# A graph-network kernel on one core: an adding transfer and a norm's use moved to later steps of the first stage

## The chip, the cores and the metric

The kernel runs on one core of a Trainium2 chip. The core has five engines that run side by side, each through its own stream of instructions in order: TensorE (PE in the profile; PEld is its weight load), VectorE (DVE), ScalarE (ACT), GpSimd (POOL) and SyncE (SP). Transfers are issued from POOL's, SP's or ACT's stream and carried out by 16 DMA engines. The metric is the time of one execution on the device, in microseconds; lower is better.

## What is computed

Four layers stand one after the other; each adds its result to its input and normalises every row of 256 values to mean 0 and variance 1. The first layer, the one that the change touches, is

```
h = relu(S @ (x @ W1)); h = relu(S @ (h @ W2)); y = S @ (h @ W3)    # S = adj * adj, 64x64
x = layernorm(x + y)          # (x - mean) / sqrt(var + 1e-5), over 256 values
```

with x of 128 x 64 x 256 values, W1 256x512, W2 512x1024, W3 1024x256, all in float32. The second layer needs the eigenvectors of a 64x64 Laplacian made from adj, applies them before and after a small two-layer network, the third holds two graph convolutions and LSTMs over windows of 1 to 4 nodes, and the fourth an attention over the graph.

## The kernel before

The 8192 rows are 64 tiles of 128 rows, in 16 groups of four tiles. The first stage (layer0) loops over the groups; layers two to four follow as a second stage, whose order a planner (class Plan, with costs and slots) decides.

**The first stage.** Each of the three products with a weight is done in the seven products of Strassen's scheme instead of eight. A generator, seven, gives one product each time that it is called by next: w2 (two of them) for the second weight, w3 for the third, w1 for the first weight of the next group. Their orders are 1, 2, 6, 5, 7, 3, 4 (w1, and w2 but for the last two) and 1, 2, 5, 6, 7, 3, 4 (w3). The result of a product is copied by ScalarE or added by VectorE out of a PSUM bank in the step after it.

The sums of operands that Strassen's scheme needs for the third weight are in the tile sh with four slots. They are made by transfers: less has ScalarE write a negated block into a slot, a plain transfer from SP copies a block, and adds (L1055) issues from POOL a transfer that adds its source to its destination. Slot 3 becomes the sum of a negated block and slot 1, and is read by w3's product 3; slot 1 is itself the result of two adding transfers.

**Steps.** The function step (L1020) is called once behind each product: it runs what is pending, that is the copy or addition of the product before, takes in a new pending piece, and then runs one piece from the list norms, if there is one:

```
if norms:
    norms.pop(0)()
```

Pieces come from mix_rows (L1122 to L1140), which multiplies by S, adds to x and puts the pieces of one half group's row norm on the list: scalar_norm (L808) gives two means (total with Identity), two sums of squares (total with Square), root (three small POOL instructions, L819 to L821) and two apply (ScalarE, L824). For the second half a piece for storing the rows follows (L1141).

**What sets the order.** Under tc.manual_schedule the streams of TensorE, VectorE and ScalarE keep the order in which the code calls them. POOL and SP are not in that list in this stage's block (it names three engines); the framework orders their streams when the program is built. The eigenvalue work of the second layer (function eigen) is spread between the products by an estimate of time; it uses TensorE, VectorE (lines L52 and L312 in the profile) and ScalarE (L385, L397) up to about 800 us.

**The hand-over.** What is left on the list norms at the end of the first stage is given to the planner of the second by left_over, one piece behind the other.

Of the kernel before, what the change touches and what calls it, by code (L numbers as in the profile page):

```python
# [12 lines left out]
AF = mybir.ActivationFunctionType  # L13
# [791 lines left out]
                                op0=ALU.subtract, op1=ALU.mult)  # L805


def scalar_norm(tc, pool, x, half, spare):  # L808


    nc = tc.nc
    S, G = nc.scalar, nc.gpsimd
    nm, va, rs, nb = (pool.tile([P, 2], F32, name=f"sn_{n}") for n in ("nm", "va", "rs", "nb"))

    def total(out, t, func, **kw):
        S.activation(spare[0](), x[:, t, :], func, accum_out=out[:, t:t + 1], **kw)

    def root():
        G.tensor_scalar(rs, va, 1.0 / D, EPS, op0=ALU.mult, op1=ALU.add)  # L819
        G.tensor_tensor(rs, rs, half[:, :2], ALU.pow)  # L820
        G.tensor_tensor(nb, nm, rs, ALU.mult)  # L821

    def apply(t):
        S.activation(x[:, t, :], x[:, t, :], AF.Identity, bias=nb[:, t:t + 1], scale=rs[:, t:t + 1])  # L824

    return ([lambda t=t: total(nm, t, AF.Identity, scale=-1.0 / D) for t in range(2)] +
            [lambda t=t: total(va, t, AF.Square, bias=nm[:, t:t + 1]) for t in range(2)] + [root] +
            [lambda t=t: apply(t) for t in range(2)])


# [6 lines left out]
def kernel(  # L837
# [58 lines left out]
    def rows_of(g):  # L896

        return X[:, 4 * g:4 * g + 4, :] if g < RING else XA[:, 4 * (g - RING):4 * (g - RING) + 4, :]
# [61 lines left out]
    eig, norms, due = [], [], [float("inf")]  # L960
# [44 lines left out]
    sh = pa.tile([P, 4, 4, 256], F32, name="sh")  # L1005
# [15 lines left out]
    def step(then=None):  # L1021

        while pending:
            pending.pop(0)()
        if then:
            pending.append(then)
        if norms:
            norms.pop(0)()
# [4 lines left out]
    def sums_of_weights(w, b12):  # L1033
        yield VL.tensor_sub(w[7], w[3], b12)
        yield VL.tensor_sub(w[5], b12, w[1])
        yield VL.tensor_sub(w[6], w[3], w[5])
        yield VL.tensor_sub(w[4], w[2], w[6])
# [9 lines left out]
    def sums_first():  # L1047
        VL.tensor_add(sx[:, 0], X21, X22)
        VL.tensor_sub(sx[:, 1], sx[:, 0], X11)
        VL.tensor_sub(X21, X11, X21)  # L1050

    def less(slot, j, c):
        S.activation(sh[:, slot, 2 * j:2 * j + 2], h2[:, 0, 4 * c + 2 * j:4 * c + 2 * j + 2, :], AF.Identity, scale=-1.0)

    def adds(out, src):  # L1055
        nc.gpsimd.dma_start(out, src, accum_op=ALU.add)  # L1056

    def burst(dst, src, c):
        to = dst.rearrange("p c (t h n) -> p h c t n", h=2, n=N)
        p = [bank().rearrange("p (c t n) -> p c t n", c=2, t=4) for _ in range(2)]  # L1060
        for t in range(4):
            for k in range(2):
                for m, f, h, hs in quads(c + k):
                    PE.matmul(p[h][m, k, t, :], src[hs, t, f], sqT2[hs, hs], start=True, stop=True)  # L1064
        now[0] += QUADS
        between()

        def result():
            for h in range(2):
                S.copy(to[:, h, c:c + 2], p[h])  # L1070

        step(result)
# [6 lines left out]
    def by_second(j):  # L1079

        def product(out, i, new):
            w, a = (x[i] for x in second)
            chained(out, [[(w[:, k, c * P:(c + 1) * P], a[:, k, :]) for k in range(2)] for c in (2 * j, 2 * j + 1)], new)

        return product
# [9 lines left out]
    def seven(n, product, c11, c12, c21, c22, last, order=(1, 2, 6, 5, 7, 3, 4)):  # L1095

        def view(b):
            return b[:, :2 * n].rearrange("p (i n) -> p i n", i=2)

        def add(dst, b):  # L1100
            VL.tensor_add(dst, dst, b)
            if last is relu:
                relu(dst, dst)

        ch = view(bank("ch"))
        for i in order:
            if i in (2, 5):
                b = view(bank("ps" if i == 2 else "b5"))
                b2, b5 = (b, None) if i == 2 else (b2, b)
            out = {2: b2 if i == 2 else None, 5: b5 if i == 5 else None, 3: b5 if i == 3 else None}.get(i, ch)  # L1110
            product(out, i, i in (1, 2, 5))
            step({1: lambda: S.copy(c11, ch), 2: lambda: add(c11, b2), 6: lambda: S.copy(c12, ch),
                  5: lambda: S.copy(c22, b5), 7: lambda: add(c22, ch), 3: lambda: add(c12, b5),
                  4: lambda: last(c21, ch)}[i])
            yield i
# [11 lines left out]
    def weigh(t):  # L1127
        p = bank()
        run(p, [(m1[:, k, t * P:(t + 1) * P], aw1[:, k, :]) for k in range(2)])
        step(lambda: relu(h1[:, t, :], p))  # L1130
# [14 lines left out]
    def sums_second():  # L1145
        S1, S2, S4 = (ss[:, i] for i in range(3))
        VL.tensor_add(S1, A21, A22)
        VL.tensor_sub(S2, S1, A11)
        VL.tensor_sub(A21, A11, A21)
        VL.tensor_sub(S4, A12, S2)  # L1150

    def layer0():
        n = NT // 4
        burst(m1, rows_of(order[0]), 0)
        step()
        for t in range(4):
            weigh(t)
            if t == 1:
                for _ in sums_of_weights(second[0], B12):
                    pass  # L1160
        step()
        for c in (0, 2):
            burst(m2, h1, c)
            step()
        for g in range(n):
            last = g == n - 1
            then = {} if last else {
                (1, 1): lambda: less(2, 0, 0),
                (1, 6): lambda: sums_first() if g else burst(m1, rows_of(order[1]), 0),
                (0, 5): lambda: (less(2, 1, 0), nc.sync.dma_start(sh[:, 1], sh[:, 2])),  # L1170
                (0, 3): lambda: (nc.sync.dma_start(sh[:, 0], H22), adds(sh[:, 1], H22)),
                (0, 4): lambda: (less(3, 0, 1), None if g else sums_first()),
                (1, 3): lambda: [adds(sh[:, slot], H21) for slot in range(3)],
            }
            sums_second()
            w2 = [seven(256, by_second(j), *[h2[:, r, 4 * c + 2 * j:4 * c + 2 * j + 2, :] for r in (0, 1) for c in (0, 1)],
                        relu, order=(1, 2, 6, 5, 7, 4, 3) if j else (1, 2, 6, 5, 7, 3, 4)) for j in range(2)]
            sums = [] if g else [signed_sums(), sums_of_weights(first[0], W12)]
            for j in (0, 0, 1, 0, 1, 0, 1, 0, 1, 1, 0, 0, 1, 1):
                then.get((j, next(w2[j])), lambda: None)()  # L1180
                for some in sums[j:]:
                    next(some, None)
            if last:
                for t in (0, 2):
                    mix_rows(g - 1, t)
                for _ in plain():
                    pass
                for t in (0, 2):
                    mix_rows(g, t)
                break  # L1190
            w3 = seven(P, by_third, *[s3[:, r:r + 2, c:c + P] for r in (0, 2) for c in (0, P)], S.copy,
                       order=(1, 2, 5, 6, 7, 3, 4))
            w1 = seven(256, by_first, *[h1[:, r:r + 2, c:c + 256] for r in (0, 2) for c in (0, 256)], relu)
            next(w3)
            less(3, 1, 1)
            adds(sh[:, 3], sh[:, 1])
            if g:
                mix_rows(g - 1, 0)
            next(w1)
            next(w3)  # L1200
            next(w1)
            VL.tensor_sub(X12, X12, sx[:, 1])
            if g:
                mix_rows(g - 1, 2)
            for w in (w1, w1, w3, w1, w3, w1, w1, w3):
                next(w)
            burst(m2, h1, 2)
            next(w3)
            burst(m2, h1, 0)
            next(w3)  # L1210
            if g + 2 < n:
                burst(m1, rows_of(order[g + 2]), 0)
        step()
# [600 lines left out]
                layer3(x, g, 0, 4)  # L1814

    def left_over():
        for piece in norms:
            plan.note("POOL" if piece.__name__ == "root" else "ACT", piece, 0.5, 0.8 * len(plan.ops))
            for first, then in zip(plan.ops[-2:], plan.ops[-1:] if len(plan.ops) > 1 else []):
                first.after.append(then)  # L1820
                then.before.add(first)
                then.left += 1
        plan.pieces = plan.ops
# [47 lines left out]
```

## Time and profile before

| what | us |
|---|---|
| median of 3 runs | 2281.51 (2278.72 to 2282.01) |
| the profiled execution | 2278.91 |
| its span | 2277.1 |
| TensorE busy in the span | 2222.8 |
| 0 to 109 us: TensorE busy | 94.27 of 109 |
| 109 to 830 us (groups with a row norm in the loop): TensorE busy | 710.29 of 721 |
| 830 to 880 us (hand-over): TensorE busy | 44.07 of 50 |
| 880 us to the end: TensorE busy | 1374.15 of 1397 |

The span runs from the first to the last instruction of one profiled execution; the runs are timed without the profiler's view, as a whole. In a line of a timeline the first number is the start from the span's begin, the second the duration, then engine, line of the kernel, operation, output and inputs by the names of the tiles; idle time before the instruction, and what ended it, stand in brackets. A line such as L52 or L162 belongs to a helper through which many instructions pass, so the tiles' names tell which it is. Of the tiles: sh holds the operand sums for the third weight, h and s are results of products (h1 and h2 are both written h), m their inputs, XA and X the rows, sn_nm, sn_va, sn_rs and sn_nb the parts of a row norm, b and ch PSUM banks, q and LV columns and a block of the eigenvalue work.

### The profile page before, as it was taken

How to read it: one execution, taken by the hardware profiler on the slowest of the kernel's cores; microseconds unless marked ns; L12 is line 12 of the kernel's file. 1: busy time of each engine (PE TensorE's matmuls, PEld its weight loads, DVE VectorE, ACT ScalarE, POOL GpSimd, SP SyncE). 2: the span in 40 equal slices, each digit the busy share in tenths (PEclk: the TensorE clock that was granted, in tenths of full speed). 3: DMA queues.
4: the chain of work that ended last, by engine and by line, in shares of the span. 5: the costliest groups of instructions: out<-in, count | busy, mean ns of one | idle time of the engine just before them, and what ended most of it. 6: DMA issues, size and time to landing. Idle time of an engine off the chain costs nothing.

```text
span 2277.1 us, 53163 instructions
## 1 busy us (share of the span) xinstructions
PE 2222.8 (98%) x20840; PEld 2025.9 (89%) x20840; DVE 1758.2 (77%) x5925; ACT 1240.5 (54%) x2999; POOL 205.2 (9%) x390
## 2 busy tenths in 40 slices
PE   7999999999999999999999999999999999999996
PEld 5888888888888878999999999999999999999985
DVE  5878787777888749765967977977877887578976
ACT  3455555454554445665655655655655656566554
POOL 0011111111111110000100000000010010000112
PEclk9999999999999999999999999999999999999998
DMA  8433333334433231000111211211211221002331
GB/s 269 91 90 75 85 75 75 84 80 97 104 75 76 65 135 48 20 1 20 66 46 43 78 59 48 87 57 43 89 62 41 77 72 33 31 29 66 112 112 50
DMA packets 95243, 163.05 MB, mean 72 GB/s; under 512 B 24976, under 2 KB 65936, under 8 KB 94992
## 3 DMA queue, kind: packets, MB, share of 16 engines
q1 hardware_dynamic: 83840, 120.05, 15.7%
q0 software_dynamic: 10800, 39.33, 9.1%
q8 instruction: 164, 2.69, 0.5%
q14 instruction: 87, 0.71, 0.1%
q10 hardware_dynamic: 352, 0.28, 0.0%
HBM read 57.64 MB, written 45.09 MB: 45 GB/s over the span
## 4 chain that ended last, share of the span: by engine, by line
PE 87%; DVE 5%; DMA 4%; ACT 2%; issue 1%; POOL 1%; SPq 0%; ACTq 0%; POOLq 0%; DVEq 0%
PE ps L162 59%; PE ch L973 13%; PE b L973 7%; PE ps L973 5%; PE ps L1064 2%; DMA sh<-h 2%; DVE D L52 1%; PE pa L312 1%; DVE h L52 1%; DMA XA<-in_x_dram 1%; DMA aw<-in_a_w_dram 1%; DVE w L162 0%; DVE tw L52 0%; DVE X L162 0%; ACT h L982 0%
## 5 line engine op out<-in xcount | busy, mean ns | idle before, releaser
L162 PE MATMUL ps<-w,wih 128*128 128x128 f32 (+2 forms) x2944 | 571.9, 298 | 1.9 <-DVE gates L162 0.7
L162 PEld LDWEIGHTS ps<-w,wih 128*128 128x128 f32 x2944 | 452.9, 191 | 28.3 <-issue 6.2
L162 PE MATMUL ps<-w,sums 128*128 128x128 f32 (+2 forms) x3104 | 476.1, 293 | 0.0
L162 PEld LDWEIGHTS ps<-w,sums 128*128 128x128 f32 x3104 | 422.8, 191 | 14.3 <-issue 1.9
L162 ACT ACTIVATE gates<-gates,cbi 128x256 f32<-128x256 f32 (+4 forms) x736 | 313.9, 479 | 173.5 <-DVE gates L162 171.5
L162 DVE TENSOR_TENSOR gates<-gates,ps 128x512 f32<-128x512 f32 (+4 forms) x408 | 233.6, 583 | 170.4 <-PE ps L162 156.5
L162 ACT COPY gates<-ps 128x512 f32<-128x512 f32 (+4 forms) x408 | 204.0, 506 | 253.1 <-PE ps L162 247.4
L982 ACT ACTIVATE h<-h 128x512 f32<-128x512 f32 x141 | 88.7, 629 | 270.6 <-DVE h L52 270.5
L162 PE MATMUL ps<-hs,whh 128*128 128x128 f32 (+1 forms) x896 | 181.2, 284 | 0.1
L162 PE MATMUL ps<-w,whh 128*128 128x128 f32 (+1 forms) x896 | 181.1, 284 | 0.0
L162 POOL TENSOR_SCALAR rs<-mv 128x2 f32<-128x2 f32 x96 | 24.1, 261 | 1321.7 <-DVE mv L162 1320.3
L162 ACT ACTIVATE gates<-ps,cbi 128x128 f32<-128x128 f32 (+2 forms) x368 | 119.1, 383 | 43.2 <-PE ps L162 42.6
L162 PEld LDWEIGHTS ps<-hs,whh 128*128 128x128 f32 x896 | 139.7, 191 | 0.3 <-DVE hs L162 0.3
L162 PEld LDWEIGHTS ps<-w,whh 128*128 128x128 f32 x896 | 139.7, 191 | 0.0
L973 PE MATMUL ch<-m,tw 128*128 128x256 f32 x512 | 120.5, 380 | 2.6 <-DVE h L52 2.6
L973 PE MATMUL b<-ss,aw 128*128 128x256 f32 x512 | 122.6, 379 | 0.0
L973 PEld LDWEIGHTS ch<-m,tw 128*128 128x128 f32 x512 | 96.3, 190 | 16.0 <-DVE h L52 3.4
L973 PEld LDWEIGHTS b<-ss,aw 128*128 128x128 f32 x512 | 96.4, 190 | 12.7
L1056 POOL DMA_DIRECT2D sh<-h x60 | 53.2, 959 | 493.7 <-PE b L973 154.4
L162 PE MATMUL ps<-hs,sums 128*128 128x128 f32 (+1 forms) x448 | 90.6, 284 | 0.0
L162 ACT ACTIVATE gates<-c 128x256 f32<-128x256 f32 (+1 forms) x176 | 75.5, 433 | 27.6 <-DVE c L162 26.2
L162 DVE TENSOR_TENSOR w<-w,w 128x128 f32<-128x128 f32 (+2 forms) x264 | 79.6, 312 | 10.7 <-PE ps L162 4.4
(384 smaller groups left out, 4275.2 us busy)
## 6 DMA issues: line engine op xcount, KB each, us to landing
sh<-h POOLq DMA_DIRECT2D x60, 512.0 KB, 5.9
far<-w SPq DMA_DIRECT2D x42, 512.0 KB, 2.7
w<-far SPq DMA_DIRECT2D x168, 128.0 KB, 3.1
X<-rest SPq DMA_DIRECT2D x24, 512.0 KB, 3.3
out_dram<-X SPq DMA_DIRECT2D x64, 128.0 KB, 1.8
sh<-sh SPq DMA_DIRECT2D x15, 512.0 KB, 2.9
sh<-h SPq DMA_DIRECT2D x15, 512.0 KB, 2.9
sh<-sh POOLq DMA_DIRECT2D x15, 512.0 KB, 4.8
```

The source lines that it names most:

```text
L52: return getattr(self.engine, name)(out, *args, **kw)
L162: getattr(e, name)(*[real(x) for x in args], **{k: real(v) for k, v in kw.items()})
L312: PE.matmul(out, lhsT, rhs, start=True, stop=True)
L973: PE.matmul(out, lhsT, rhs, start=start, stop=stop, **kw)
L982: S.activation(dst, src, AF.Relu)
L1056: nc.gpsimd.dma_start(out, src, accum_op=ALU.add)
L1064: PE.matmul(p[h][m, k, t, :], src[hs, t, f], sqT2[hs, hs], start=True, stop=True)
```

## The change

Two edits in the first stage. The adding transfer of slot 3 (adds(sh[:, 3], sh[:, 1])) moves, in the code, from behind w3's first product to behind w1's fourth call, which is its product 5. The list of a row norm gets an empty piece, skip, between root and the two applies, so that one step passes in which no piece of the norm is issued; left_over drops these empty pieces.

```diff
+def skip():
+    pass
...
-            [lambda t=t: total(va, t, AF.Square, bias=nm[:, t:t + 1]) for t in range(2)] + [root] +
+            [lambda t=t: total(va, t, AF.Square, bias=nm[:, t:t + 1]) for t in range(2)] + [root, skip] +
             [lambda t=t: apply(t) for t in range(2)])
...
             next(w3)
             less(3, 1, 1)
-            adds(sh[:, 3], sh[:, 1])
             if g:
                 mix_rows(g - 1, 0)
             next(w1)
...
             if g:
                 mix_rows(g - 1, 2)
-            for w in (w1, w1, w3, w1, w3, w1, w1, w3):
+            next(w1)
+            next(w1)
+            adds(sh[:, 3], sh[:, 1])
+            for w in (w3, w1, w3, w1, w1, w3):
                 next(w)
...
-        for piece in norms:
+        for piece in [x for x in norms if x is not skip]:
```

## The prediction

> **What bounds the kernel.** The page comes first: 2277.1 us of span inside a profiled execution of 2278.91 us.
>
> ```profile
> span 2277.1 us, 53163 instructions
> PE 2222.8 (98%) x20840; PEld 2025.9 (89%) x20840; DVE 1758.2 (77%) x5925; ACT 1240.5 (54%) x2999; POOL 205.2 (9%) x390
> ```
>
> TensorE (PE) is busy for 98%: anything taken off another engine counts only where TensorE stood waiting for it. Both edits lie in the first stage, so the next view is who waited, for POOL and then ScalarE (ACT), from 0 or 100 to 790 us (total us, times, longest).
>
> ```profile
> POOL sn_rs L819 <- ACT spare L816: 85.7, 18, 8.1
> POOL sh L1056 <- DMA sh<-h: 34.1, 16, 8.3
> ...
> ACT XA L824 <- POOL sn_nb L821: 28.7, 24, 4.3
> ```
>
> ScalarE lost 28.7 us at the first "apply" of a row norm, usually near 0.9 us but once 4.3. What of that reaches TensorE is a third view, TensorE's own waits in the same window, and it is little:
>
> ```profile
> PE ch L973 <- DVE h L52: 4.7, 5, 1.6
> PE b L973 <- ACT h L1113: 2.8, 2, 1.5
> PE ch L973 <- ACT s L1112: 1.1, 5, 0.3
> PE pa L312 <- DVE LV L52: 0.5, 1, 0.5
> ```
>
> The large ones stand in two of the groups, at 170 to 173 us and at 426 to 429 us. The timeline of the first (start, duration, instruction, idle before it and its releaser):
>
> ```profile
> 166.84 0.87 POOL L1056 DMA_DIRECT2D sh<-sh  x1 [8.32 <-DMA sh<-h]
> 168.86 0.20 POOL L821 TENSOR_TENSOR sn_nb<-sn_nm,sn_rs 128x2 f32<-128x2 f32 x1
> 169.09 0.60 ACT L824 ACTIVATE XA<-XA,sn_nb,sn_rs 128x256 f32<-128x256 f32 x1 [3.98 <-POOL sn_nb L821]
> 169.59 0.56 ACT L1113 COPY h<-b 128x512 f32<-128x512 f32 x1
> 170.21 1.13 PE L973 MATMUL b<-aw,m 128*128 128x256 f32 x4 [1.46 <-ACT h L1113]
> 171.37 0.19 ACT L397 ACTIVATE q<-q 64x1 f32<-64x1 f32 x1
> 171.59 0.15 DVE L52 RECIPROCAL q<-q 64x1 f32<-64x1 f32 x1 [4.17 <-ACT q L397]
> 172.22 0.68 DVE L52 TENSOR_TENSOR h<-h,ch 128x512 f32<-128x512 f32 x1
> 172.95 1.13 PE L973 MATMUL ch<-tu,m 128*128 128x256 f32 x4 [1.61 <-DVE h L52]
> ```
>
> Read it downward. POOL holds the adding transfer of sh[:, 3] until an earlier adding transfer, issued at 157.64, has landed near 166; the norm's root is queued behind it; the apply on ScalarE waits for the root; and the copy h<-b, ready since about 165, is queued behind the apply. TensorE needs that copy (1.46 us), then an addition on VectorE (DVE), which itself stands behind the eigenvalue chain's reciprocal, waiting for a ScalarE root q (1.61 us). The group at 411 to 464 us repeats it to the hundredth: apply at 424.99, q at 427.27, waits of 1.38 and 1.61.
>
> [...] the trace has a median of 4.8 us from issue to landing for this transfer, which I use.
>
> **The change, part by part.**
>
> *The moved transfer.* In the code it goes behind two more products of the first weight. But only TensorE, VectorE and ScalarE run in the order of the code in this stage; POOL and SP are ordered when the program is built. I compared the two built programs: POOL's stream is the same, instruction by instruction and wait by wait, and so is SP's. The transfer still stands directly ahead of the root. Its issue takes 0.86 us of POOL as before, x15, and no queue sees it at another place. Cost and gain 0. If the compared order were not what runs, the bound is easy: the root first would release the apply at about 166.1 (its last total ends 164.64, root 1.3) and could save the whole wait of both groups, 2 x 3.1 = 6.2 us; against it, in a group like that at 515 us the transfer would go from 523.00 to 527.1 and land near 532.8 (issue 0.86 and 4.8), still ahead of its reader at 535.88: no loss.
>
> *The empty step.* It moves ScalarE's instructions only (VectorE and TensorE differ in a handful of rows after 830 us). In each of 14 groups the first apply stands behind the copy h<-b instead of ahead of it, the second behind s<-b, the first mean total of the next rows behind the relu of h, and the second pair of applies behind two copies each. Nothing is added: an empty step issues nothing.
>
> In the two stalled groups, POOL's release at 169.09 stays. Ahead of q there were, by the distances between starts: apply 0.50, h<-b 0.47, apply 0.50, a constant copy 0.13, s<-b 0.27, mean total 0.41, together 2.28. Now apply 0.50, constant copy 0.13, s<-b 0.27, apply 0.50, together 1.40. So q comes 0.88 us earlier, and with it reciprocal, addition, and TensorE's product (172.95 to 172.07). The first wait (1.46) disappears, because h<-b no longer stands behind the apply, but TensorE then only reaches the second sooner: from 168.6 plus 0.86 it waits until 172.07, some 2.6 us. The stall shrinks by 0.88, not by 3.07. Two groups: -1.8 us.
>
> In the group at 261 us TensorE waited 0.50 for LV and 0.33 for the addition, both behind the same reciprocal. There q follows the apply (270.93) by 1.62; with the constant copy and h<-b ahead of the apply it follows by 0.50, 1.12 earlier. That clears 0.83; I keep 0.7, since the wait for s<-ch just after (0.19) may grow by 0.1. In the group at 208 us the 0.62 stays: VectorE ran without a gap from 220.70 on, released by TensorE, not by ScalarE. The other waits for s<-ch (0.19 to 0.28) stay, since relu, one mean total and s<-ch keep their distance. The second square total (0.49) now stands ahead of the burst's copies; in the groups without eigenvalue work these wait for the burst itself (copies at 584.24, burst ended 584.18, the total would end near 583.2), and in the others they lose the apply's wait for POOL (0.75 to 0.93) in return. Cover gone, 0.49 in each group would be at stake; TensorE took none of these waits before. 0, with +1 as the bad end.
>
> *The hand-over at 830 us.* One piece more of the last norms is left over for the next stage: 21 for 20. ScalarE's second square total now precedes its second w<-ps copy, 0.5 us later; VectorE's w copy at 834.20 covers it. The v activations come 0.0 to 0.2 later and TensorE has waits on them (0.30, 0.24). The last applies, ended 848.27, would end near 850.4, TensorE wanting those rows at 850.51 and after. I take +0.2, from -0.5 to +2.
>
> Sum: -1.8 - 0.7 + 0.2 = -2.3 us. Nothing later absorbs it: TensorE is busy 98% from 880 us to the end. The profiled execution would be 2278.91 - 2.3 = 2276.6; the median shown lies 2.6 above that execution, so the forecast is 2281.51 - 2.3 = 2279.2. The three runs spread over 3.3 us, more than the effect.
>
> **Rivals.** (a) *The whole stall goes*: 2 x 3.1 and 0.7, about -6.7, 2274.8. It needs POOL to run the root ahead of the transfer, or the addition on VectorE to be ahead of the reciprocal. The built orders speak against both. (b) *Nothing reaches TensorE*: 2281.5, if the late transfer lands later still, or run-to-run shifts eat it. For it: the effect is smaller than the spread. (c) *Slower, by the hand-over*: each left-over norm goes ScalarE, POOL root (0.19 + 0.69 + 0.20 and the distances, about 1.3), ScalarE again, and four such rounds run between 830 and 848. If each slipped by 1.5 to 2.3 instead of 0.5 in all, the last applies would be 6 to 9 late against a margin of 850.51 - 848.27 = 2.2, and TensorE would stand 4 to 7 us; with the 2.5 gained above it ends at +1.5 to +4.5, up to 2286. It decides from a slip of 4.7 us on (2.2 + 2.5). Against it: ScalarE has 5.4 and 5.8 us of idle at 816 to 828, and the reordered rows are few.
>
> **Chances.** The likeliest 0.60, (a) 0.14, (b) 0.15, (c) 0.11. The bound of 0.2% is 4.6 us, about what a measurement of this kernel can tell from no change: faster means below 2276.9, slower above 2286.1. From the likeliest, 0.10 of its 0.60 falls below by spread, and 0.01 above; (a) gives 0.11 of its 0.14; (b) 0.01 below and 0.02 above; (c) 0.06 above. Together faster 0.22, same 0.69, slower 0.09. The likeliest's own range is 2276.7 to 2281.7; taking in (b), most of (a) and part of (c), 2275.0 to 2283.5.
>
> **What would show it.** Right: POOL's transfer still directly ahead of the root, at about 167 and 423 us, with 8 us of idle; h<-b ahead of the apply; TensorE's waits for h L1113 gone, those for DVE h L52 in the two groups grown to about 2.6 each; q about 0.9 earlier. Wrong: a root ahead of the transfer, waits of both kinds gone, or TensorE waiting for s L1113 or m L1070, or for X at 850 us.

## The result and the profile after

The changed kernel takes 2276.47 us, the median of 17 runs (2272.1 to 2278.37), against 2281.51 us for the kernel before (17 runs beside them, 2277.95 to 2285.07). The ratio is 0.9977 with a 95% interval of 0.997 to 0.9985, which is 5.2 us less (3.4 to 6.8). The forecast was 2.3 us less: the sign and the range held, the size was too small. The profiled execution of the changed kernel took 2277.01 us, 1.9 less than that of before. The head of its page:

```profile
span 2275.2 us, 53164 instructions
PE 2223.6 (98%) x20840; PEld 2026.8 (89%) x20840; DVE 1758.3 (77%) x5925; ACT 1241.5 (55%) x2999; POOL 203.6 (9%) x390
```

The same work is done: the counts of each engine are those of before. So the time can only have come from waits or from TensorE's clock, of which more below. ScalarE's wait at the apply, and below it TensorE's own waits, both from 100 to 790 us of the changed kernel (total us, times, longest):

```profile
ACT XA L828 <- POOL sn_nb L825: 13.5, 15, 3.5
```

```profile
PE ch L977 <- DVE h L52: 5.4, 4, 2.4
PE ch L977 <- ACT s L1116: 1.1, 5, 0.3
PE ch L977 <- ACT h L986: 1.0, 1, 1.0
```

The lines are four higher than in the code of before: L1113 is now L1117, L973 is L977, L1056 is L1060. ScalarE waits 13.5 us for the root instead of 28.7. Of this TensorE sees little. Its wait for the copy h<-b (2.8 us) and that for LV (0.5) are gone, while that for VectorE's addition to h went up, from 4.7 to 5.4. The timeline of the group at 158 us of the changed kernel shows why:

```profile
167.67 0.87 POOL L1060 DMA_DIRECT2D sh<-sh  x1 [8.32 <-DMA sh<-h]
169.67 0.20 POOL L825 TENSOR_TENSOR sn_nb<-sn_nm,sn_rs 128x2 f32<-128x2 f32 x1
169.90 0.60 ACT L828 ACTIVATE XA<-XA,sn_nb,sn_rs 128x256 f32<-128x256 f32 x1 [3.47 <-POOL sn_nb L825]
171.31 0.19 ACT L397 ACTIVATE q<-q 64x1 f32<-64x1 f32 x1
171.53 0.16 DVE L52 RECIPROCAL q<-q 64x1 f32<-64x1 f32 x1 [3.28 <-ACT q L397]
172.16 0.67 DVE L52 TENSOR_TENSOR h<-h,ch 128x512 f32<-128x512 f32 x1
172.89 1.13 PE L977 MATMUL ch<-tu,m 128*128 128x256 f32 x4 [2.44 <-DVE h L52]
```

POOL's transfer still stands directly ahead of the root, with the same 8.32 us of idle; this execution is 0.83 us later than that of before by the time it reaches this group. The copy h<-b no longer stands behind the apply: it started at 165.84. But q, the ScalarE root in the eigenvalue chain, does, 1.41 us behind the apply's start (169.90 to 171.31) where it was 2.28. TensorE gets the first product at once and then stands 2.44 us at the second.

Because both kernels have the same 20840 weight loads on TensorE in the same order (but for two that swap places at the hand-over), their traces can be laid on each other, load by load. Where the distance between the two changes, time was won or lost. From here on a "step" is such a change of the distance; it leaves out whatever happened earlier in the execution. The changed kernel has -0.89 us in the group at 158 us, -1.13 in that at 261, and -0.37 at 832 to 837 us. In the group at 411 us it is -1.41, read where TensorE's wait ends; right after it, from 427.45 to 430.86 us, the profile shows TensorE's granted clock at 0.50, and over that stretch the distance goes back by 1.56 us. The wait itself:

```profile
426.25 1.13 PE L977 MATMUL ch<-tu,m 128*128 128x256 f32 x4 [1.85 <-DVE h L52]
```

### The profile page after: what moved, and what is told of

Read it like the earlier page. It is cut to its first block, busy times and chain, and to the rows that moved or that the text cites. A ratio compares the mean times of both kernels' runs of the same rounds, so it can differ in the third digit from the quotient of the medians.

```text
span 2275.2 us, 53164 instructions
## 1 busy us (share of the span) xinstructions
PE 2223.6 (98%) x20840; PEld 2026.8 (89%) x20840; DVE 1758.3 (77%) x5925; ACT 1241.5 (55%) x2999; POOL 203.6 (9%) x390
## 4 chain that ended last, share of the span: by engine, by line
PE 88%; DVE 5%; DMA 3%; ACT 1%; issue 1%; SPq 1%; POOL 1%; ACTq 0%; POOLq 0%; DVEq 0%
PE ps L162 59%; PE ch L977 14%; PE b L977 7%; PE ps L977 5%; PE ps L1068 2%; DMA sh<-h 1%; DVE D L52 1%; PE pa L312 1%; DMA XA<-in_x_dram 1%; DVE h L52 1%; DVE w L162 0%; DVE tw L52 0%; SPq L921 0%; DVE gates L162 0%; DVE X L162 0%
## 5 line engine op out<-in xcount | busy, mean ns | idle before, releaser
L977 PE MATMUL ch<-m,tw 128*128 128x256 f32 x512 | 120.6, 380 | 3.0 <-DVE h L52 3.0
L977 PE MATMUL b<-ss,aw 128*128 128x256 f32 x512 | 122.7, 379 | 0.0
L977 PEld LDWEIGHTS ch<-m,tw 128*128 128x128 f32 x512 | 96.2, 190 | 16.6 <-DVE h L52 4.0
L977 PEld LDWEIGHTS b<-ss,aw 128*128 128x128 f32 x512 | 96.4, 190 | 12.7
L1060 POOL DMA_DIRECT2D sh<-h x60 | 53.1, 956 | 483.1 <-PE b L977 150.0
```

What stands on the lines that cost most here:

```text
L977: PE.matmul(out, lhsT, rhs, start=start, stop=stop, **kw)
```

## The experiments

All times are medians beside runs of the kernel before on the same chip; those runs had medians of 2280.16 us (each edit alone, and the first two with POOL in the code's order), 2279.86 (the empty step in some groups only, and slot 1 third), 2280.68 (the next three) and 2279.92 (the last one). A difference in us is worked out from the ratio and that median, unless it is said otherwise.

**The moved transfer alone.**

```diff
             less(3, 1, 1)
-            adds(sh[:, 3], sh[:, 1])
...
+            next(w1)
+            next(w1)
+            adds(sh[:, 3], sh[:, 1])
+            for w in (w3, w1, w3, w1, w1, w3):
```

> Only the adding transfer is moved in the code; no empty step. Theory (the framework orders POOL, so the move changes nothing): all five streams of the built program equal those of the kernel before, so 0 us, ratio 1.000, with TensorE's waits of about 1.4 and 1.6 us at 170 to 173 and 426 to 429 us in place. Rival (the move itself brings part of the gain): -1 us or more, POOL's root ahead of the transfer.

2280.19 us, ratio 1.0002 (0.9994 to 1.0011). The streams of all five engines are those of before, row by row. The first edit does nothing, and this run is also a measure of what the comparison gives for no change.

**The empty step alone.**

```diff
-            ... + [root] +
+            ... + [root, skip] +
...
-        for piece in norms:
+        for piece in [x for x in norms if x is not skip]:
```

> Only the empty step; the transfer stays where it was in the code. Theory: the streams equal those of the changed kernel, so the whole of its gain, -3 to -5 us (ratio 0.9978 to 0.9987), waits for h<-b gone and the addition's wait 1.8 to 2.5 us in the two groups. Rival: less than the changed kernel by what the move brings, at least 1 us.

2277.87 us, ratio 0.9987 (0.9981 to 0.9994), 3.0 us less (1.4 to 4.3). Its streams are those of the changed kernel. The steps of its trace are -1.17 (158 us), -1.12 (261), -1.13 (411, again read ahead of slower products: from 427.06 us on sixteen of ch<-tv,sh took 3.65 us, where sixteen at 420.81 took 1.95) and -0.37 (hand-over). So the whole effect is the empty step's.

**The empty step in three half groups only**, those whose norms run in the groups at 158, 261 and 411 us; and **everywhere else**. With `g in (1, 3, 6) and not t` as the condition for the first:

```diff
-            norms.extend(scalar_norm(tc, small, x2, half, spare))
+            norms.extend(x for x in scalar_norm(tc, small, x2, half, spare) if x is not skip or (g in (1, 3, 6) and not t))
```

> The kernel before, with the empty step in three half groups only: the first halves normed in the groups at 158, 261 and 411 us. The streams of the built program differ from before by 36 rows of ScalarE and nothing else; the hand-over is as before. Theory (the gain is made where TensorE stood behind the apply): nearly all of it, -3.0 us (0.9 + 1.1 + 1.0), ratio 0.9987. Rival (many small gains over 14 groups, or the hand-over): -1 us or less.

> The complement: the empty step everywhere but in those three half groups, the hand-over as in the changed kernel. Theory: the three stalls stay as before (1.4 and 1.6 us twice, 0.5 and 0.3 once), the hand-over gives -0.4, so 0 to -0.5 us, ratio 1.000. Rival: -2 us or more.

In the three: 2277.75 us, 0.9993 (0.9986 to 0.9999), 1.6 us less (0.2 to 3.2). The steps are -0.88, -1.11 and -1.01, and none elsewhere; their sum, -3.0, is what was expected and lies inside the interval of the timing, near its end. The span of this profiled execution is 2277.8 us at a mean granted clock of 0.994, that of before 2277.1 at 0.996. Elsewhere: 2279.44 us, 0.9999 (0.999 to 1.0007), with -0.4 at the hand-over. At 158 and 411 us its trace gains 0.3 each too, but there slot 3's transfer left POOL 0.3 earlier, and the moved transfer alone, with the streams of before, shows the same -0.33 at 411 us. By the traces, then, the gain lies in those three groups and the hand-over, and the other groups take and give nothing; the timing alone could not have told.

**POOL in the code's order.** The stalls come from POOL's order, which the framework chooses. Naming POOL in the list of engines that keep the code's order brings the root ahead of the transfer in the changed kernel, which is the prediction's rival (a) made true:

```diff
-    with tc.manual_schedule(engines={mybir.EngineType.PE, mybir.EngineType.DVE, mybir.EngineType.Activation}):
+    with tc.manual_schedule(engines={mybir.EngineType.PE, mybir.EngineType.DVE, mybir.EngineType.Activation, mybir.EngineType.Pool}):
```

> The changed kernel, with POOL's stream too in the order of the code in the first stage, so that the root of the first norm stands ahead of the adding transfer. Theory (the rest of the stall is the root queued behind the transfer): TensorE's waits of 2.4 and 1.9 us at 173 and 426 us go, the apply starts 1.4 us after the last total, a further -3 to -4.5 us against the changed kernel, -7 to -9 against before. Rival (VectorE's eigenvalue chain or the transfer's later landing takes its place): less than 1 us more than the changed kernel, with a wait for sh before w3's product 3.

2268.98 us, 0.9943 (0.9929 to 0.9956), 13.0 us less (10.0 to 16.2) where 7 to 9 were expected, which makes it the fastest kernel of this study. From its timeline:

```profile
164.34 0.20 POOL L825 TENSOR_TENSOR sn_nb<-sn_nm,sn_rs 128x2 f32<-128x2 f32 x1
164.57 0.60 ACT L828 ACTIVATE XA<-XA,sn_nb,sn_rs 128x256 f32<-128x256 f32 x1 [0.43 <-POOL sn_nb L825]
164.97 0.92 POOL L1060 DMA_DIRECT2D sh<-sh  x1 [0.43 <-PE b L977]
167.99 1.03 PE L977 MATMUL ch<-tu,m 128*128 128x256 f32 x4
```

The apply waits 0.43 us, the transfer leaves behind the root, and TensorE's product has no wait at all. The steps: -1.4 in the first group (52 to 106 us), -3.8 at 158, -1.1 at 261, -3.8 at 411, -0.4 at the hand-over. Their sum is -10.5. The first group's 1.4 is a wait of 1.1 us at w3's product 5 for the adding transfer of slot 0, which the framework had put second there, behind slot 2's; the code's order also removes it.

**The same order without the change.** With the same line in the kernel before, the transfer stays ahead of the root, since the code of before calls it there.

> The kernel before, with POOL's stream in the order of the code: the transfer ahead of the root in every group, and the three adding transfers of the second block in the order slot 0, 1, 2 in every group. Theory (the two late groups are late because the framework had put slot 1 last there, so the transfer waits for the last of three): slot 1 is then the second of three, the transfer is free about 2 us earlier, and the stall of 3.1 us per group shrinks to about 1: -3 to -4 us. Rival (the lateness is of those places in time, not of the order): same as before, 0.

2272.59 us, 0.9963 (0.995 to 0.9975), 8.4 less (5.7 to 11.4): twice what was expected. From its timeline:

```profile
163.61 0.87 POOL L1056 DMA_DIRECT2D sh<-sh  x1 [5.11 <-PE b L973]
165.85 0.60 ACT L824 ACTIVATE XA<-XA,sn_nb,sn_rs 128x256 f32<-128x256 f32 x1 [1.56 <-POOL sn_nb L821]
169.72 1.13 PE L973 MATMUL ch<-tu,m 128*128 128x256 f32 x4 [0.92 <-DVE h L52]
```

The transfer of slot 3 leaves at 163.61 instead of 166.84 although the root is still behind it. (The profile names a product as what it waited for last; but slot 1's transfer landed at 162.90, 0.71 us ahead of it, and in the kernel before at 166.13, again 0.71 ahead.) What differs is ahead of it: three adding transfers of the second block, for the slots 0, 1 and 2, are called at one point of the code, and the framework had put that of slot 1, the one which slot 3's transfer reads, third in the first group and in those at 158 and 411 us (the order there is 2, 0, 1, to be told from the semaphores that each transfer waits for). In the code's order slot 1 is second everywhere. Steps: -1.4, -2.4 and -3.0 in these three groups, -6.8 in all; the first group's is the wait for slot 0 again. In the two stalled groups, with the two traces laid on each other, slot 3's transfer leaves POOL 2.41 and 3.02 us earlier, which is the whole step. So the late landing of slot 1 makes 2.4 and 3.0 of the 3.8 us that a stalled group costs, and the root's place behind slot 3's transfer passes it on to TensorE.

**Slot 1 third in every group**, without and with the empty step: the suspected cause multiplied.

```diff
-                (1, 3): lambda: [adds(sh[:, slot], H21) for slot in range(3)],
+                (1, 3): lambda: [adds(sh[:, slot], H21) for slot in (0, 2, 1)],
```

(and POOL in the code's order).

> The kernel before, POOL in the order of the code, and the three adding transfers of the second block in the order slot 0, 2, 1 in every group, so that the transfer into slot 3 always waits for the last one issued. Theory (this order makes the root late, whatever the group): POOL holds the transfer until about 8 us after the last issue in all 14 groups, the apply and h<-b come 2 to 4 us late in all of them, TensorE loses 1.4 to 3.1 us in each: +15 to +35 us against before. Rival (only those two places in time are late): within 4 us of before.

> The same with the empty step. Theory: h<-b is free in every group; what remains of the stall is the addition behind the eigenvalue chain's root, in the 8 groups with eigenvalue work up to 560 us, and none in the 6 after, so about half of the loss of the run without the step is won back, 8 to 20 us. Rival (the stall only moves to the next wait, as it did in the two groups of the changed kernel): less than 0.9 us in each group, at most 12 us in all, and the last 6 groups slow too.

Without: 2294.87 us, 1.007 (1.0055 to 1.0085), 16 slower. With: 2284.02, 1.0017 (1.001 to 1.0024), 4 slower; by the medians the empty step wins back 10.9 us here, of which, by an estimate from the slope in the last experiment, about 1.7 go with a lower clock of the first (0.9928 against 0.9945). TensorE's waits from 100 to 790 us, first without:

```profile
PE b L973 <- ACT h L1113: 6.8, 7, 1.4
PE ch L973 <- DVE h L52: 4.6, 5, 1.6
PE ch L973 <- ACT s L1112: 3.7, 10, 0.6
```

and with the empty step:

```profile
PE ch L977 <- ACT s L1116: 6.0, 11, 1.4
PE ch L977 <- DVE h L52: 6.0, 5, 2.4
```

Without the empty step the stall of h<-b comes in seven groups of this window and an eighth at 792 us, and not in all 14 as was expected; the 16 us are at the low end of the forecast. With it that wait is gone in all eight, as the theory says. But the expectation that the last six groups, which have no eigenvalue work, would then lose nothing was wrong: three of them lose 1.3 to 1.7 each, with waits of 1.1 to 1.4 at the copy s<-ch (L1116), which now stands behind the two late applies and a relu. As at 158 us, the empty step moves one copy ahead of a late apply and leaves a later use behind it.

**Slot 1 first**, in the changed kernel, once with POOL ordered by the framework and once in the code's order:

```diff
-                (1, 3): lambda: [adds(sh[:, slot], H21) for slot in range(3)],
+                (1, 3): lambda: [adds(sh[:, slot], H21) for slot in (1, 0, 2)],
```

> The changed kernel, with the three adding transfers of the second block called in the order slot 1, slot 0, slot 2 instead of 0, 1, 2; POOL is still ordered by the framework, which here too leaves the transfer of slot 3 ahead of the root. Theory (the apply is late because the framework puts slot 1's adding transfer third in the groups at 158 and 411 us, so that it lands late and slot 3's transfer holds up the root behind it): the transfer of slot 3 leaves POOL 3 us or more earlier there, TensorE's waits for DVE h L52 of 2.4 and 1.9 shrink to below 0.3, and so does the wait in the first group; 8 to 10 us below the kernel before, 4 to 6 below the changed kernel. Rival (the place of the root behind the transfer is what costs, whatever lands first): as the changed kernel, 4 to 5 us below before.

> Both edits of the change, POOL's stream in the code's order, and slot 1's adding transfer first of the three. Theory (code order alone already gives slot 1 time enough): within 1 us of the same kernel with the slots in the order 0, 1, 2, so 10.5 to 12 below before. Rival (slot 3 still lands late enough somewhere to hold TensorE): 13 or more below before.

Both missed, theory and rival alike: 2284.92 us, 1.0018 (1.0011 to 1.0026), and 2282.59, 1.0003 (0.9994 to 1.0011). TensorE's waits of the first, from the start to 900 us, and its group at 411 us:

```profile
PE b L977 <- DMA sh<-h: 11.6, 9, 2.2
PE ch L977 <- DVE h L52: 3.5, 3, 2.4
```

```profile
431.17 2.05 PE L977 MATMUL b<-tv,sh 128*128 128x128 f32 x16 [1.36 <-DMA sh<-h]
```

The half of the theory that concerns the stalls held: the waits for the addition in the groups at 158 and 411 us are gone (the longest of the three that are left stands at 52 us). A new wait of 11.6 us in nine groups took their place, and it was to be read in the code: w3's products come in the order 1, 2, 5, and product 5 reads slot 0, before any product reads slot 1. Slot 0's transfer now stands behind slot 1's second addition, and that one waits until slot 1's first has landed. In the group at 158 us of the first run this landing comes at 165.64, slot 0's transfer leaves at 166.56 and lands at 174.57, and product 5 starts at 174.61. The first group of the kernel before, with its wait for slot 0, had shown the same in small. The order 0, 1, 2 of the code serves both readers.

**The moved transfer in the code's order, without the empty step.** With POOL ordered by the code the first edit does move something, and this tells what the empty step is still worth then.

> The moved transfer and POOL's stream in the code's order, without the empty step. POOL then runs the root ahead of the transfer. Theory (with the root early, the apply no longer comes late in the two stalled groups, and the empty step keeps only the 1.1 of the group at 261 us and the 0.4 of the hand-over): 1.5 us slower than the same with the empty step (11.2 below before), so 9 to 10.5 below before. Rival (the empty step is worth nothing once the root is early): 11 below before.

2273.91 us, 0.9966 (0.9954 to 0.9979), 7.8 less. From its timeline:

```profile
167.14 0.92 POOL L1056 DMA_DIRECT2D sh<-sh  x1 [0.43 <-PE b L973]
170.60 1.13 PE L973 MATMUL ch<-tu,m 128*128 128x256 f32 x4 [0.27 <-DVE h L52]
271.72 0.46 PE L312 MATMUL pa<-AQ,LV 128*128 128x128 f32 x2 [0.49 <-DVE LV L52]
```

The steps are -1.4 in the first group, -3.1 at 158, 0 at 261, -3.4 at 411 and 0 at the hand-over. Beside POOL in the code's order with both edits (-3.8, -1.1, -3.8, -0.4 after the first group) the empty step is still worth 2.7 us by the trace, more than the 1.5 expected: 0.8 and 0.4 come from the two stalled groups, where, in the first of them, 0.27 us of wait stays without it. The ratios are 5 us apart, but their intervals touch, so they don't speak against the 2.7.

**The changed kernel once more**, for the size.

> The changed kernel itself once more. If its size is the sum of the steps that the traces show one by one (0.9 in the group at 158 us, 1.1 at 261, 1.0 to 1.4 at 411, 0.3 to 0.4 at the hand-over), it lies 3 to 4 us below the kernel before. If the first comparison had the size right, 5 us below. If the forecast had it, 2.3.

2275.59 us, 0.9978 (0.997 to 0.9987), 5.0 less (3.0 to 6.8): the first comparison's size again, which the sum of the changed kernel's steps, 3.8 (0.89, 1.13, 1.41 and 0.37), doesn't reach. The same streams have now been timed three times, at 5.2, 3.0 and 5.0 us less. Part of the rest goes with the clock. Within one kernel, runs with a mean granted clock lower by 0.001 are about 1 us longer (0.8 to 1.2 for the kernel before in the several comparisons). In this last comparison the kernel before had a mean of 0.9938 and a mean span of 2278.6 us, the changed one 0.9950 and 2273.8: of the 4.9, by an estimate from that slope, some 1.2 go with the clock and 3.7 remain. For the empty step alone the clocks were nearly the same (0.9940 and 0.9942), and 2.6 of 2.8 remain. By the steps and at like clocks, then, the change is worth 2.6 to 3.8 us. The two runs with POOL in the code's order had a better clock too, 0.9954 with the change and 0.9960 without it against 0.9940, so that, by the same estimate, some 1.4 of their 13.0 and 2 of their 8.4 us go with it; their steps sum to 10.5 and 6.8. Why the same streams had a better clock in one comparison than in the other stays open, and the clocks of before in the very first comparison are not listed, so that its 5.2 can't be split in this way.

## Why the prediction was right, and where it was off

- *The moved transfer, 0*: right. The streams are the same and the time is the same (1.0002). That it was the built order which runs, and not the code's, is shown by the row of POOL at 167.67.
- *First wait gone, second grown to 2.6, net -0.88 in a stalled group*: right. The second wait is 2.44, q follows the apply by 1.41 where 1.40 was worked out, and the group gained 0.89 in the changed kernel and 1.17 in the empty step alone. In the group at 411 us q follows by 1.41 too (423.26 to 424.67), and the wait is 1.85 only, since slot 3's transfer left POOL 0.52 us earlier there, after 7.9 us of idle instead of 8.5. That part of the gain is a transfer's spread and not the change's. It accounts for all the difference between traces: in both groups of the changed kernel, of its repetition, of the empty step alone and of the three half groups the steps lie between 0.88 and 1.41, slot 3's transfer leaves 0 to 0.52 earlier, and the one less the other is 0.87 to 0.89 all eight times.
- *The group at 261 us, -0.7*: the mechanism right, the term too small: -1.13, -1.12 and -1.11 in three traces. It was made from TensorE's wait rows, 0.50 and 0.33. The weight load's rows say more. Of the kernel before, and then of the changed one:

```profile
275.73 0.73 PEld L973 LDWEIGHTS ch<-tu,m 128*128 128x128 f32 x4 [0.73 <-DVE h L52]
275.74 1.13 PE L973 MATMUL ch<-tu,m 128*128 128x256 f32 x4 [0.33 <-DVE h L52]
```

```profile
274.53 0.73 PEld L977 LDWEIGHTS ch<-tu,m 128*128 128x128 f32 x4 [0.34 <-DVE h L52]
274.54 1.13 PE L977 MATMUL ch<-tu,m 128*128 128x256 f32 x4
```

  In both pairs the load starts 0.01 us ahead of the product, and in the first both waited for the same event; in the changed kernel with POOL in the code's order, where this line waited for nothing, the load started 0.21 us ahead (167.78 and 167.99). So the load's row shows 0.40 us more of the stall than the product's. The load's wait fell from 0.73 to 0.34, and that for LV, 0.66 in the load's row, went wholly: 1.05, near the 1.12 measured.
- *The hand-over, +0.2*: the wrong sign, -0.37. The step was "the v activations come 0.0 to 0.2 later". They come earlier, because the empty pieces leave the left-over pieces in another place of the planner's order: one v activation moved between the two applies, where it had stood behind both. The waits for v of 0.30 and 0.24 became one of 0.21. The -0.37 is alike in all traces with the empty step in the last groups; read on to 870 us, the whole hand-over is between -0.26 and -0.72 in them. Rival (c), which built on this place, had no part of it.
- *Rival (a)*: it did not happen in the changed kernel, and when it was made to happen it was worth more than its price, 3.8 for each stalled group and not 3.1. The missing 0.7 is again the exposed load: in the group at 158 us of the kernel before the rows of the weight load show waits of 1.65, 2.01 and 0.16, together 3.82, where the products show 1.46 and 1.61.
- *The sum*: -2.3 against a sum of steps of -3.8: 0.4 from the group at 261, 0.6 from the hand-over's sign, and 0.5 from the earlier landing at 411, which is chance; without it the sum is -3.3. The medians' -5.2 and -5.0 are beyond both, more than twice the forecast, with the clock as a part of what lies between. The rest is not explained.
- *What the prediction did not ask*: why slot 3's transfer was held until 166 us at all. It took the landing of 8.5 us as given. The cause was the order of the three transfers before it, which was as much the framework's choice as the root's place, and worth more than the change: 8.4 us by the timing, 6.8 by the steps, without touching either edit.

## What to carry to other kernels

Where an engine's queue is ordered by the framework, moving a call in the code may move nothing: read the built order, and look there first for the transfer that is waited for and for what was put ahead of it. An empty step that lets independent copies pass a late use is worth the part of the lateness that nothing else behind that use brings back; here 0.9 of the 3.8 that a stalled group lost, while the code's order for POOL, with the change, won back all of it. When several transfers are issued together, their order has to follow all their readers, the one that reads next and the one that starts the next chain.

## What the runs showed of the hardware

- Three adding transfers of 512 KB that POOL issued at 155.15, 155.70 and 157.64 us of the kernel before landed 4.98, 7.10 and 8.49 us after their own starts. The median of this line is 5.9 on its page, and 2.9 for SP's plain copies of the same size. From 156 to 165 us of the changed kernel, with adding transfers in flight, the 16 DMA engines moved 175 to 229 GB/s in each slice of 0.75 us; with one of SP's plain copies in flight beside an adding transfer the highest slice was 415 in the same trace and 404 in the run with slot 1 first. In the kernel before with POOL in the code's order, where slot 1 is the second of the three everywhere, the steps sum to 6.8 us.
- In the profiled execution of the kernel before the granted clock was 0.50 from 846.12 to 849.53 us, from 2235.34 to 2238.75, from 2245.58 to 2248.99 and from 2269.47 to the end; in that of the changed kernel from 427.45 to 430.86, from 2233.10 to 2239.93 and from 2263.82 to the end. The one at 427.45 us took back 1.56 us of the distance between the two traces, which is of the size of the effect studied; so steps were read from traces and not from the end of a span alone.
- In the changed kernel the stretch at 427.45 us follows a wait of TensorE of 1.85 us that ended at 426.25. Waits of 2.44 us (to 172.89) and 2.66 us (to 845.67) in the same trace are followed by none: the clock was 1.00 from 173 to 176 and from 846 to 849.4 us. What brings such a stretch about was not shown.
